# Selecting experts' tokens: counts of the later pairs through DRAM, the residual copied behind the first gathers, steps placed by distance

## The chip, the cores and the metric

The kernel runs on one core of a Trainium2 chip. A core has TensorE (PE), VectorE (DVE), ScalarE (ACT), GpSimd (POOL) and SyncE (SP), each with its own instruction stream, and 16 DMA engines that all queues share. The metric is device microseconds of one execution; less is better. Compared are medians of several executions.

## The reference

A block of three layers on x of 4 x 2048 tokens (8192 in all) of 256 floats: half of a mixture of experts, an attention, half of the same mixture of experts, each on the layer norm of x and added to x.

```python
x = x + 0.5 * ffn(layernorm(x));  x = x + attn(layernorm(x));  x = x + 0.5 * ffn(layernorm(x))

def ffn(x):                      # E = 8 experts, K = 2, capacity = 1.25 * 8192 / 8 = 1280
    probs = softmax(x @ router_w.T)
    topw, topi = top_k(probs, 2);  topw = topw / (sum(topw) + 1e-6)
    # of each expert's tokens the `capacity` with the largest weight are kept
    g, u = disp @ wg, disp @ wu  # per expert: 1280 x 256 @ 256 x 1024
    eo = (silu(g) * u) @ wd      # 1280 x 1024 @ 1024 x 256
    return sum over kept (token, expert) of weight * eo
```

The attention has 16 heads and is linear in the number of tokens (a context of keys and values, then queries times the context).

## The kernel before

**Stages.** A first router (layer norm, logits, the two best experts, their weights), then the first eight experts, the attention (with the second router's work in its last part), and the second eight experts. Each expert stage is `experts`, called twice.

**Experts.** An expert's 1280 tokens are two chunks of 640, so there are chunks 0 to 15; an even chunk is an expert's first half. For each chunk, tokens' rows are gathered from DRAM by five indirect DMAs of 128 rows (`gather`, L775, on GpSimd's queue), scaled on ScalarE (`norm`, L790; for chunk 0 on VectorE, L788), transposed (`turn`) and multiplied (`units`, TensorE at L899; then `down`, L1114) in a scheme with fewer block products and sums before and after, which run on VectorE (L840) and GpSimd (L843). Results are added to rows in DRAM by indirect DMAs (`send_tile`, L1048): into `acc` in the first stage, into the output in the second. `units` goes through four column blocks p = 0 to 3; near the third `ct` sum of each stands the place that the change calls "fifth", a little later (not for p = 3) the place "fourth", and `down` has one place, "end". Each place is a call of `aside`, which does one step of the pairs' work below. Before, "fifth" is used in odd chunks only.

**Which tokens an expert keeps.** Experts are treated in pairs. To find the 1280th largest weight of each of a pair's experts, a search with 7 + 7 rounds (`ROUNDS`, upper and lower half of the float's bits) compares 512 numbers of each partition to a threshold of that partition and counts. A partition is one of 8 `MARKS` groups (2 experts x 4 thresholds) of 16 partitions; the counts of a group's 16 partitions must be summed and be known on all partitions, as all derive the next thresholds from them. `Pair.steps` is a generator: each `yield` ends one step. A round is `sign` (ScalarE: signs of all keys less the threshold, summed per partition into `part`, a half float, L432) and `turn` (TensorE: `part` as a weight, broadcast, times the group matrix `own_b`, into a `reach` bank in PSUM, L436; VectorE: compare with `MOST_ABOVE` into `seen` and `ahead`, L437, and move the threshold `mark`, L440). After the rounds come the tail's steps: ties and larger ones (L496, L497), sums over partitions on TensorE (L505) and a scan on VectorE (L391), places (L509 to L514), a transpose back (`back`, L517) and the slots (L519, L486 to L488), from which the lists of rows are made.

The first pair (experts 0, 1) has its own code in `route`. The other three are `Pair`s 1 to 3 of `Others`, one after the other: 24 steps each, 72 in all. `route` does eight of them, `first_list` one and `first_turn` three; of the other 60, an expert's two chunks take twelve (four in the even chunk, eight in the odd one). The list of expert 2, the first of pair 1, is made in chunk 2, that of expert 4 in chunk 6, of expert 6 in chunk 10.

**Order.** Inside `tc.manual_schedule` the order on TensorE, VectorE, ScalarE (and GpSimd in the routers) is that of the code. SP is ordered by a planner. SP issues all plain loads and stores: x, the weights (`load_expert`: `wgt`, `wut`, `wdt`, 1 MB each, two experts' buffers), the rows and `acc`. Each DMA of SP also waits for the one that used its semaphore before. A DMA that waits holds up what is behind it on SP.

**The residual.** `acc` begins as a copy of x: four stores of 2 MB from `xw` in SBUF (L1622), three ahead of the rows' four stores (L388), one behind them; then `wdt` of expert 0 (`load_down`). The rows, 280 floats per token, are what the gathers read.

Of the kernel before, what the change touches and what calls it, by code (L numbers as in the profile page):

```python
# [20 lines left out]
P = 128  # L21
# [7 lines left out]
def macaron_kernel(  # L29
# [40 lines left out]
    acc = dram.tile([B * N, D], F32, name="acc")  # L70

# [85 lines left out]
    LONE = float(1 << 14)  # L157
    ACROSS = P * SEG

    def marks_of(name, weight, lacks):  # L160
# [13 lines left out]
    own_b = const.tile([P, MARKS + 1], F16, name="own_b")  # L174
    nc.gpsimd.memset(own_b, 0.0)
    nc.gpsimd.tensor_copy(own_b[:, :MARKS], heads[:, :: P // MARKS])
# [11 lines left out]
    rungs_a, rungs_b = (  # L188
        const.tile([P, len(UNITS), ROUNDS, MARKS + 1], F32, name=f"rungs_{k}") for k in "ab"
    )  # L190
    moves = const.tile([P, len(UNITS), ROUNDS + 2], F32, name="moves")
    for part, unit in enumerate(UNITS):
        strides = [unit * (COPIES + 1) ** (ROUNDS - 1 - n) for n in range(ROUNDS)] + [0.0]
        for n in range(ROUNDS):
            nc.gpsimd.memset(rungs_a[:, part, n, :], strides[n])
            nc.gpsimd.tensor_scalar(
                rungs_b[:, part, n, :MARKS], half_of[:, :: P // MARKS], strides[n], None, ALU.mult
            )
            nc.gpsimd.memset(moves[:, part, n : n + 1], strides[n + 1] - strides[n])
        nc.gpsimd.memset(moves[:, part, ROUNDS:], strides[0])  # L200
# [4 lines left out]
    nc.gpsimd.tensor_copy(rungs_b[:, :, :, MARKS:], moves[:, :, :ROUNDS].unsqueeze(3))  # L205
# [17 lines left out]
    shift = const.tile([P, T], F32, name="shift")  # L223
    slot_lo = const.tile([P, E, T], I16, name="slot_lo")
# [168 lines left out]
    class Pair:  # L393
# [4 lines left out]
        def use(self, pool, ppool, tag, bufs=1):  # L398
            self.pool, self.ppool, self.tag, self.bufs = pool, ppool, tag, bufs

# [25 lines left out]

        def steps(self):

            s, mark = self.s, self.s["mark"]

            def sign(key):
                nc.scalar.activation(self.junk, key, AF.Sign, bias=mark, scale=-1.0, accum_out=s["part"])  # L432

            def turn(half, n):
                reach = self.bank("reach")[:, : MARKS + 1]
                nc.tensor.matmul(reach, s["part"].to_broadcast([P, P]), own_b, start=True, stop=True)  # L436
                nc.vector.scalar_tensor_tensor(  # L437
                    s["seen"], reach, MOST_ABOVE, rungs_b[:, half, n, :], ALU.is_le, ALU.mult, accum_out=s["ahead"]
                )
                nc.vector.tensor_scalar(mark, s["ahead"], mark, None, ALU.add)  # L440

            es = slice(self.e - PAIR, self.e)
            w0 = self.key.rearrange("p (r m) -> p r m", r=QT)
            for e in range(PAIR):
                nc.scalar.copy(
                    w0.rearrange("p r (e g q) -> p r e g q", e=PAIR, g=COPIES)[:, :, e],
                    spread(
                        raw[:, self.e - PAIR + e, :].rearrange("p (q r) -> p r q", r=QT).unsqueeze(2),
                        [P, QT, COPIES, T // QT],
                    ),  # L450
                )
# [5 lines left out]
            nc.scalar.mul(self.key, low, UNITS[1])  # L457
            with nc.allow_low_precision(reason="sums of at most 512 signs are exact in half floats"):
                sign(upper)
                yield  # L460
                for n in range(ROUNDS - 1):
                    turn(0, n)
                    sign(upper)
                    yield
                turn(0, ROUNDS - 1)
                nc.vector.tensor_scalar(s["high"], mark, 0.5, None, ALU.add)
                yield
                nc.vector.tensor_scalar(s["top"], s["high"], float(1 << 16), None, ALU.mult)
                nc.vector.scalar_tensor_tensor(self.key, upper, s["high"], self.key, ALU.subtract, ALU.add)
                nc.vector.tensor_copy(mark, moves[:, 1, ROUNDS + 1 :])  # L470
                yield
                sign(self.key)
                yield
                for n in range(ROUNDS - 1):
                    turn(1, n)
                    sign(self.key)
                    yield
# [3 lines left out]
            yield  # L481
# [7 lines left out]
            yield  # L489

        def tail(self, wt):
# [6 lines left out]
            yield  # L498
# [9 lines left out]
            yield  # L508
# [6 lines left out]
            yield  # L515
# [6 lines left out]
            yield  # L522

    class Others:
# [8 lines left out]

        def step(self):
            next(self.left, None)

    def route(w, w0, pool, ppool, sums=iter(()), beside=iter(())):
# [51 lines left out]
        for n, _ in enumerate(first.tail(pair)):  # L589
            if n == 2:  # L590
# [128 lines left out]
    def load_down(e, weights):  # L719
        nc.sync.dma_start(out=weights[e][2], in_=wd[e].rearrange("(f p) d -> p f d", p=P))  # L720

    def load_expert(e, wpool, weights, behind=(), whole=True):
# [9 lines left out]
        if whole:  # L732
            load_down(e, weights)
# [22 lines left out]
    def experts(name, src, dst, wait_for, others, weights, ws, wpool, lpool, pool, ppool):  # L756
# [131 lines left out]
        def units(k):  # L888
# [82 lines left out]
            for p in range(NF):  # L971
# [13 lines left out]
                if k % PER:  # L985
                    aside(k)
                if not last:
# [11 lines left out]
                    aside(k)  # L999
# [40 lines left out]
        def aside(k):  # L1040

            others.step()
# [50 lines left out]
        def down(k, hs):  # L1093
# [56 lines left out]
            aside(k)  # L1150
# [29 lines left out]
        with tc.manual_schedule(engines=ENGINES - {mybir.EngineType.Pool}):  # L1180
# [402 lines left out]
    with tc.tile_pool(name="w1", bufs=2) as wpool:  # L1583
        weights, ws = {}, {}
        read = tc.alloc_tile_pool(name="read", bufs=1, side="right")
        with tc.tile_pool(name="r1", bufs=1) as pool, tc.tile_pool(name="r1p", bufs=2, space=PSUM) as ppool:
# [99 lines left out]
```

## Time and profile before

| what | us |
|---|---|
| median of three runs (lowest, highest) | 1976.41 (1975.58, 1977.82) |
| the profiled execution, its span | 1976.69, 1974.9 |
| first router and first lists, to the first product of chunk 0 (L899) | 0 to 96.2 |
| first expert stage, to the end of its last scatter-add | 96.2 to 893.4 |
| attention | to 1119.6 |
| second selection, to its first product | to 1169.0 |
| second expert stage | 1169.0 to the end |

The page's first part gives each engine's busy time, the fourth the chain of work that ended last. The granted TensorE clock is 0.971 of full on average. Windows give the busy time of each engine in a stretch; timelines the single instructions, with the idle time before and what ended it in square brackets. L numbers are lines of the kernel before.

### The profile page before, as it was taken

The numbers are of one execution on the slowest core, as the hardware profiler recorded it, in microseconds if no ns is written. First come the engines' busy times: TensorE is split into PE (matmuls) and PEld (weight loads), VectorE is DVE, ScalarE is ACT, GpSimd is POOL, SyncE is SP. The second block draws the span as 40 slices with busy tenths as digits, with TensorE's granted clock in tenths as the row PEclk, the third lists the DMA queues.
The fourth block names the chain that finished last, engine by engine and source line by source line (L and its number), as shares of the span: only waits on it lengthen the run. The fifth ranks groups of instructions, "written<-read, shape, count | busy, mean of one in ns | idle before, by whom it ended". The sixth has DMA issues, their size and how long they took to land.

```text
span 1974.9 us, 26091 instructions
## 1 busy us (share of the span) xinstructions
PE 1866.0 (94%) x8882; PEld 1338.4 (68%) x8882; DVE 1372.7 (70%) x2677; ACT 1030.4 (52%) x2598; POOL 1030.3 (52%) x1061
## 2 busy tenths in 40 slices
PE   7499999999999999999999659999999999999997
PEld 5366766676667777776888536666666666777776
DVE  8678677776777676646677667867686767676763
ACT  5273747374736463325566437374737473737332
POOL 6434555555555555535555435555545554555552
PEclk9599999999999999999999869999999999999999
DMA  9912232222222221115012541313131313132121
GB/s 346 308 50 75 46 74 47 71 50 71 50 71 50 71 50 28 29 22 178 22 43 90 201 160 18 92 25 96 22 90 26 95 26 88 30 96 28 31 28 19
DMA packets 108005, 148.90 MB, mean 75 GB/s; under 512 B 7512, under 2 KB 94560, under 8 KB 107872
## 3 DMA queue, kind: packets, MB, share of 16 engines
q1 hardware_dynamic: 76992, 103.16, 15.3%
q0 software_dynamic: 30720, 43.93, 13.7%
q8 instruction: 70, 1.15, 0.2%
q14 instruction: 63, 0.52, 0.1%
q10 hardware_dynamic: 160, 0.14, 0.1%
HBM read 91.11 MB, written 56.10 MB: 75 GB/s over the span
## 4 chain that ended last, share of the span: by engine, by line
PE 46%; DVE 4%; ACT 2%; issue 1%; POOL 1%; DMA 1%; POOLq 0%; SPq 0%; DVEq 0%; ACTq 0%
PE mm L899 23%; PE mm L1114 11%; PE py L1412 3%; PE pc L1354 3%; PE qp L1295 3%; DVE ct L840 1%; PE back L1066 1%; PE tr L801 1%; PE trq L1342 1%; DVE junk_a L562 1%; PE trx L1287 1%; DVE key L514 0%; PE ix L699 0%; ACT lo L693 0%; POOL out_dram L1048 0%
## 5 line engine op out<-in xcount | busy, mean ns | idle before, releaser
L899 PE MATMUL mm<-xs,ws 128*128 128x320 f32 x1536 | 479.3, 435 | 1.7 <-DVE u L840 1.7
L843 POOL TENSOR_TENSOR ct<-ct 128x320 f32<-128x320 f32 x360 | 337.0, 936 | 200.9 <-DVE ct L930 151.7
L899 PEld LDWEIGHTS mm<-xs,ws 128*128 128x128 f32 x1536 | 282.2, 190 | 116.8 <-DVE ct L840 6.6
L840 DVE TENSOR_TENSOR ct<-u,mm 128x640 f32<-128x640 f32 x256 | 209.5, 819 | 151.3 <-PE mm L899 110.5
L775 POOL DMA_INDIRECT r<-rows,ixs x160 | 156.6, 979 | 273.3 <-ACT eo L1047 197.1
L927 ACT ACTIVATE ct<-ct 128x960 f32<-128x960 f32 (+1 forms) x192 | 141.2, 735 | 299.2 <-DVE ct L840 285.9
L840 DVE TENSOR_TENSOR ct<-ct,mm 128x640 f32<-128x640 f32 x288 | 236.0, 819 | 72.9 <-PE mm L899 57.2
L1114 PE MATMUL mm<-ct,wds 128*128 128x320 f32 x960 | 279.6, 433 | 1.0 <-DVE ct L840 1.0
L693 ACT ACTIVATE lo<-from_below,behind_lo 128x129 f16<-128x129 f16 x896 | 272.8, 395 | 0.0
L1114 PEld LDWEIGHTS mm<-ct,wds 128*128 128x128 f32 x960 | 178.7, 190 | 75.0 <-DVE ct L840 7.0
L1114 PE MATMUL mm<-ct,wdt 128*128 128x320 f32 x720 | 217.2, 438 | 0.0
L1048 POOL DMA_INDIRECT acc<-eo,ixs x80 | 128.0, 1600 | 146.4 <-ACT eo L1047 128.4
L1048 POOL DMA_INDIRECT out_dram<-eo,ixs x80 | 127.9, 1599 | 146.3 <-ACT eo L1047 128.4
L899 PE MATMUL mm<-xsT,wgt 128*128 128x320 f32 x512 | 189.9, 453 | 3.0 <-ACT p L939 2.0
L899 PE MATMUL mm<-xsT,wut 128*128 128x320 f32 x512 | 179.6, 432 | 0.0
L930 DVE TENSOR_TENSOR ct<-ct 128x640 f32<-128x640 f32 (+1 forms) x128 | 158.1, 1235 | 22.0 <-ACT ct L927 22.0
L1114 PEld LDWEIGHTS mm<-ct,wdt 128*128 128x128 f32 x720 | 133.4, 193 | 49.3 <-issue 4.2
L840 DVE TENSOR_TENSOR u<-p,mm 128x640 f32<-128x640 f32 x126 | 103.4, 821 | 87.6 <-PE mm L899 56.1
L899 PE MATMUL mm<-xsT,ws 128*128 128x320 f32 x512 | 161.8, 439 | 2.4 <-DVE ct L840 2.4
L939 ACT COPY p<-mm 128x640 f32<-128x640 f32 x126 | 86.4, 686 | 90.1 <-PE mm L899 74.5
L899 PEld LDWEIGHTS mm<-xsT,ws 128*128 128x128 f32 x512 | 97.4, 191 | 43.9 <-DVE ct L840 4.3
L899 PEld LDWEIGHTS mm<-xsT,wut 128*128 128x128 f32 x512 | 97.3, 190 | 40.6 <-issue 0.2
(340 smaller groups left out, 2932.9 us busy)
## 6 DMA issues: line engine op xcount, KB each, us to landing
wgt<-in_L_ffn_wg_dram SPq DMA_DIRECT2D x16, 1024.0 KB
wut<-in_L_ffn_wu_dram SPq DMA_DIRECT2D x16, 1024.0 KB
wdt<-in_L_ffn_wd_dram SPq DMA_DIRECT2D x16, 1024.0 KB
rows<-xw SPq DMA_DIRECT2D x6, 2240.0 KB
xw<-in_L_attn_x_dram SPq DMA_DIRECT2D x16, 512.0 KB
acc<-xw SPq DMA_DIRECT2D x4, 2048.0 KB
out_dram<-xw SPq DMA_DIRECT2D x16, 512.0 KB
xw<-acc SPq DMA_DIRECT2D x15, 512.0 KB
```

Source lines behind the costliest of these rows:

```text
L693: nc.scalar.activation(lo[:, t, :], from_below, AF.Sign, bias=at, scale=1.0)
L775: gathers[k].append(nc.gpsimd.indirect_dma_start(out=r, out_offset=None, in_=src[:, :], in_offset=bass.IndirectOffsetOnAxis(ap=lists[e][:, ...
L840: nc.vector.tensor_tensor(o, a, b, op)
L843: nc.gpsimd.tensor_tensor(o, a, b, op)
L899: nc.tensor.matmul(ps, a, b, start=start, stop=True, skip_group_check=not start)
L927: nc.scalar.activation(h(p)[:, qs, :], h(p)[:, qs, :], AF.Silu)
L930: engine.tensor_tensor(h(p)[:, qs, :], h(p)[:, qs, :], hT(p)[:, qs, :], ALU.mult)
L939: nc.scalar.copy(p1, ps)
L1048: ins = nc.gpsimd.indirect_dma_start(out=dst[:, :], out_offset=bass.IndirectOffsetOnAxis(ap=lists[e][:, i0 + i : i0 + i + 1], axis=0), in_ ...
L1114: nc.tensor.matmul(ps, a(p), b(p), start=(p == 0 and not more), stop=(p == NF - 1), skip_group_check=more)
L1295: nc.tensor.matmul(qp[i][:, k, 0:W1], xT[i][:, k, c, :], wqx[:, c, :], start=(c == 0), stop=(c == DC - 1))
L1354: nc.tensor.matmul(pcs[b][:, c, 0 : D + 1], eks[i][:, k, c * P : (c + 1) * P], ring[i % 4][:, k, :], start=(first and k == 0), stop=(last ...
```

## The change

Of pairs 2 and 3 (`far`), a round's counts go another way: SP stores `part` (one half float of each of 128 partitions) into a DRAM tile `told`, then loads those 128 half floats to every partition, into `heard` (memory of `shift`, free at that time). `turn` sums them by groups on VectorE (into memory of `rstd`) and compares that sum, now in SBUF, instead of the PSUM bank. For pair 1 the matmul stays. A ninth column (`MARKS + 1`), which had carried the threshold's own move through the compare, is gone; the move is now a second operand of the instruction that moves `mark`. Two small set-up operations of GpSimd go with it.

Each `yield` now says how far off the next step should be (3, 7 or, after a far sign, 7.5), and `aside` knows each place's distance from the chunk's start (chunks counted as 49.0); a step is done at the first place that is not nearer than that. "fifth" is a place in all chunks. Two pairs of steps are joined (`low` with the copy, sums with places), so a pair has 23 steps.

`acc` is copied from x in DRAM to DRAM, four DMAs that wait for the gathers of chunk 0. The planner's order on SP is now: x and small weights; `wgt`, `wut`, `wdt` of expert 0; `wut`, `wdt` of expert 1; the rows' four stores; the four copies; `wgt` of experts 1 and 2; and from there stores and loads of `told` between the weights. Of the 28 rounds of a stage, those of pair 2 begin at the end of chunk 1 and finish in chunk 4, those of pair 3 run in chunks 6 to 9. In each stage the wait of `wdt` of experts 3 and 5 stands ahead of one store of `told` (those after the steps at the "end" of chunks 3 and 7).

```diff
+    told = dram.tile([1, P], F16, name="told")
...
+    ROUND = 7.5
...
+    heard = shift.bitcast(F16)[:, :P]
...
+        def far_step(self):
+            return ROUND if self.called else 3
+
         def steps(self):
 
             s, mark = self.s, self.s["mark"]
+
+            def reached():
+                if not self.called:
+                    reach = self.bank("reach")[:, :MARKS]
+                    nc.tensor.matmul(reach, s["part"].to_broadcast([P, P]), own_b, start=True, stop=True)
+                    return reach
+                reach = rstd[:, :MARKS]
+                nc.vector.tensor_reduce(reach, heard.rearrange("p (m k) -> p m k", m=MARKS), AX.X, ALU.add)
+                return reach
 
             def sign(key):
                 nc.scalar.activation(self.junk, key, AF.Sign, bias=mark, scale=-1.0, accum_out=s["part"])
+                self.called = self.far
+                if self.far:
+                    nc.sync.dma_start(out=told.rearrange("o p -> p o"), in_=s["part"])
+                    nc.sync.dma_start(out=heard, in_=told[0, :].partition_broadcast(P))
 
             def turn(half, n):
-                reach = self.bank("reach")[:, : MARKS + 1]
-                nc.tensor.matmul(reach, s["part"].to_broadcast([P, P]), own_b, start=True, stop=True)
                 nc.vector.scalar_tensor_tensor(
-                    s["seen"], reach, MOST_ABOVE, rungs_b[:, half, n, :], ALU.is_le, ALU.mult, accum_out=s["ahead"]
+                    s["seen"][:, :MARKS], reached(), MOST_ABOVE, rungs_b[:, half, n, :], ALU.is_le, ALU.mult,
+                    accum_out=s["ahead"],
                 )
-                nc.vector.tensor_scalar(mark, s["ahead"], mark, None, ALU.add)
+                nc.vector.tensor_scalar(mark, s["ahead"], mark, moves[:, half, n : n + 1], ALU.add, ALU.add)
...
-                yield
+                    yield self.far_step()
...
             scan(place, tie)
-            yield
             nc.vector.tensor_copy(nums, cnt)
...
+        def start(self):
+            self.due = 0.0
+            for pair in self.pairs[1:]:
+                pair.far = True
+
         def step(self):
-            next(self.left, None)
+            return next(self.left, None)
+
+        def step_at(self, at):
+            if at >= self.due:
+                self.due = at + (self.step() or 0.0)
...
-                if k % PER:
-                    aside(k)
+                aside(k, "fifth", p)
...
-        def aside(k):
+        PLACES = {"fifth": (7.3, 15.2, 23.2, 31.0), "fourth": (10.6, 18.6, 26.6), "end": (45.8,)}
+
+        def aside(k, place, p=0):
 
-            others.step()
+            others.step_at(k * 49.0 + PLACES[place][p])
...
             if 1 not in weights:
+                for b in range(B):
+                    some = slice(b * N, (b + 1) * N)
+                    after(nc.sync.dma_start(out=acc[some, :], in_=x_rows[some, :]), gathers[0], "the first rows come first")
                 load_expert(1, wpool, weights, gathers[0])
             first_turn()
+            others.start()
...
-            load_expert(0, wpool, weights, whole=False)
+            load_expert(0, wpool, weights)
...
-                batches = [slice(b * NJ, (b + 1) * NJ) for b in range(B)]
-                for n, b in enumerate(batches[: B - 1] + batches + batches[B - 1 :]):
-                    if B - 1 <= n < 2 * B - 1:
-                        write_rows(xw, rows[0], b)
-                    else:
-                        nc.sync.dma_start(out=acc_tiles[:, b, :], in_=xw[:, b, 0:D])
-                load_down(0, weights)
+                for b in range(B):
+                    write_rows(xw, rows[0], slice(b * NJ, (b + 1) * NJ))
```

More of the change, by code (lines that the diff above doesn't have):

```diff
@@ L173, in macaron_kernel @@
     marks_a = marks_of("a", LONE, (-(CAP - 1.0) * LONE / ACROSS,) * 2)
-    own_b = const.tile([P, MARKS + 1], F16, name="own_b")
-    nc.gpsimd.memset(own_b, 0.0)
-    nc.gpsimd.tensor_copy(own_b[:, :MARKS], heads[:, :: P // MARKS])
+    own_b = const.tile([P, MARKS], F16, name="own_b")
+    nc.gpsimd.tensor_copy(own_b, heads[:, :: P // MARKS])
     MOST_ABOVE = B * N - 2.0 * CAP + 1.0
@@ L187, in macaron_kernel @@
     nc.vector.tensor_reduce(which, inside, AX.X, ALU.add)
-    rungs_a, rungs_b = (
-        const.tile([P, len(UNITS), ROUNDS, MARKS + 1], F32, name=f"rungs_{k}") for k in "ab"
-    )
+    rungs_a = const.tile([P, len(UNITS), ROUNDS, MARKS + 1], F32, name="rungs_a")
+    rungs_b = const.tile([P, len(UNITS), ROUNDS, MARKS], F32, name="rungs_b")
     moves = const.tile([P, len(UNITS), ROUNDS + 2], F32, name="moves")
@@ L196, in macaron_kernel @@
             nc.gpsimd.tensor_scalar(
-                rungs_b[:, part, n, :MARKS], half_of[:, :: P // MARKS], strides[n], None, ALU.mult
+                rungs_b[:, part, n, :], half_of[:, :: P // MARKS], strides[n], None, ALU.mult
             )
@@ L204, in macaron_kernel @@
     )
-    nc.gpsimd.tensor_copy(rungs_b[:, :, :, MARKS:], moves[:, :, :ROUNDS].unsqueeze(3))
     for part, unit in enumerate(UNITS):
@@ L399, in use @@
             self.pool, self.ppool, self.tag, self.bufs = pool, ppool, tag, bufs
+            self.far = False
         def bank(self, name):
@@ L451, in steps @@
                 )
-            yield
+            yield 7
             high, low = self.copies(w0, self.bank("copies"))
@@ L455, in steps @@
             nc.scalar.copy(upper, high)
-            yield
             nc.scalar.mul(self.key, low, UNITS[1])
+            yield 3
             with nc.allow_low_precision(reason="sums of at most 512 signs are exact in half floats"):
                 sign(upper)
-                yield
+                yield self.far_step()
                 for n in range(ROUNDS - 1):
@@ L463, in steps @@
                     sign(upper)
-                    yield
+                    yield self.far_step()
                 turn(0, ROUNDS - 1)
                 nc.vector.tensor_scalar(s["high"], mark, 0.5, None, ALU.add)
-                yield
+                yield 3
                 nc.vector.tensor_scalar(s["top"], s["high"], float(1 << 16), None, ALU.mult)
@@ L470, in steps @@
                 nc.vector.tensor_copy(mark, moves[:, 1, ROUNDS + 1 :])
-                yield
+                yield 3
                 sign(self.key)
-                yield
+                yield self.far_step()
                 for n in range(ROUNDS - 1):
@@ L476, in steps @@
                     sign(self.key)
-                    yield
+                    yield self.far_step()
                 turn(1, ROUNDS - 1)
@@ L480, in steps @@
             nc.vector.tensor_tensor(s["cand"], s["cand"], s["top"], ALU.bitwise_or)
-            yield
+            yield 3
             ps = self.bank("pair")[:, :P]
@@ L488, in steps @@
             nc.scalar.activation(behind_lo[:, es], slot_lo[:, es], AF.Identity, bias=a_half, scale=-1.0)
-            yield
+            yield 3
         def tail(self, wt):
@@ L497, in tail @@
             nc.vector.tensor_scalar(above, wt, cand, 0.0, ALU.is_gt, ALU.add, accum_out=parts[:, 0:1])
-            yield
+            yield 7
             cnt = self.bank("all")[:, :2]
@@ L507, in tail @@
             scan(place, tie)
-            yield
             nc.vector.tensor_copy(nums, cnt)
@@ L514, in tail @@
             nc.vector.scalar_tensor_tensor(place, place, off, above, ALU.add, ALU.mult)
-            yield
+            yield 7
             ps = self.bank("back")[:, :P]
@@ L521, in tail @@
             )
-            yield
+            yield 3
     class Others:
@@ L589, in route @@
         for n, _ in enumerate(first.tail(pair)):
-            if n == 2:
+            if n == 1:
                 others.step()
@@ L717, in end, with load_expert @@
             return ix
-    def load_down(e, weights):
-        nc.sync.dma_start(out=weights[e][2], in_=wd[e].rearrange("(f p) d -> p f d", p=P))
-    def load_expert(e, wpool, weights, behind=(), whole=True):
+    def load_expert(e, wpool, weights, behind=()):
         if e >= E:
@@ L731, in load_expert @@
         weights[e] = wgt, wut, wdt
-        if whole:
-            load_down(e, weights)
+        nc.sync.dma_start(out=wdt, in_=wd[e].rearrange("(f p) d -> p f d", p=P))
     NF = FC // 2
@@ L998, in units @@
                     silu(p, slice(1, 4))
-                    aside(k)
+                    aside(k, "fourth", p)
                     if not ahead:
@@ L1149, in down @@
             sums_of_x(k + 1)
-            aside(k)
+            aside(k, "end")
             p4 = banks()[:, 0, :BH]
```

## The prediction

> **What bounds the kernel now.** I read the page first: span 1974.9 us, and the profiled execution took 1976.69 us, 0.28 over the median of 1976.41; so the sum below starts from 1976.7.
>
> ```profile
> PE 1866.0 (94%) x8882; PEld 1338.4 (68%) x8882; DVE 1372.7 (70%) x2677; ACT 1030.4 (52%) x2598; POOL 1030.3 (52%) x1061
> ...
> PE 46%; DVE 4%; ACT 2%; issue 1%; POOL 1%; DMA 1%; POOLq 0%; SPq 0%; DVEq 0%; ACTq 0%
> PE mm L899 23%; PE mm L1114 11%; PE py L1412 3%; PE pc L1354 3%; PE qp L1295 3%; DVE ct L840 1%; PE back L1066 1%; PE tr L801 1%; PE trq L1342 1%; DVE junk_a L562 1%; PE trx L1287 1%; DVE key L514 0%; PE ix L699 0%; ACT lo L693 0%; POOL out_dram L1048 0%
> ```
>
> TensorE carries the two expert stages. A change to the later pairs' steps counts only by the TensorE time it takes, or by making TensorE wait. To price the steps I laid four chunks side by side in the windows view, each from the middle of one down product to the middle of the next (chunks 4, 5, 12, 13 of the first stage; columns: TensorE, its weight load, VectorE, ScalarE, GpSimd busy, clock, DMA share, GB/s).
>
> ```profile
> 286.41:335.67 49.26, 48.66 (x193) 33.83 (x193) 36.78 (x61) 30.87 (x83) 27.07 (x23) 1.00 0.24 50
> 335.67:388.20 52.53, 50.61 (x266) 34.96 (x265) 38.28 (x72) 25.80 (x65) 26.05 (x23) 1.00 0.27 67
> 686.90:734.55 47.65, 47.65 (x189) 33.61 (x188) 35.43 (x52) 28.06 (x75) 27.35 (x23) 1.00 0.25 52
> 734.55:783.58 49.03, 49.03 (x254) 34.68 (x254) 31.72 (x44) 23.71 (x59) 26.85 (x23) 1.00 0.17 29
> ```
>
> The last two have no steps: TensorE never idles, 47.65 us for an even chunk, 49.03 for an odd one. Measured so (by the starts of the copy at L1133), chunks 1 to 9 of the first stage exceed these by 3.50, 0.65, 1.13, 1.61, 3.48, 0.74, 1.15, 1.61, 5.17 = 19.0 us, those of the second by 20.5. This 39.5 us is all that steps cost there. Most lies in the three chunks per stage that end a pair (25.9 us in six). The timelines of VectorE, GpSimd and TensorE show how:
>
> ```profile
> 175.38 1.11 DVE L391 TENSOR_TENSOR_SCAN key<-ones,scratch 128x128 f32<-128x128 f32 x1
> 176.53 2.79 DVE L514 SCALAR_TENSOR_TENSOR key<-key,nums_b,scratch 128x128 f32<-128x128 f32 x1
> ```
> ```profile
> 176.16 3.01 POOL L930 TENSOR_TENSOR ct<-ct 128x1280 f32<-128x1280 f32 x1
> ```
> ```profile
> 179.38 0.33 PE L517 MATMUL back<-ident,key 128*128 128x128 f32 x1 [1.52 <-DVE key L514]
> 180.11 1.34 PE L899 MATMUL mm<-xsT,ws 128*128 128x320 f32 x4 [0.41 <-DVE ct L840]
> ```
>
> VectorE takes `key` beside GpSimd and needs 2.79 us (0.35 in the first pair's tail, with GpSimd idle); the transpose of it is the next step, 3 us later in TensorE's order, so TensorE waits 1.52 + 0.41. In three of the six the next six matmuls then took 3.0 instead of 1.6 us, with the granted clock at 0.50: an idle of 2 us can cost 1.5 more.
>
> A count on TensorE costs little: the eight of chunk 3 cost 1.13 us, 0.14 each.
>
> **The change, part by part.**
>
> *Counts through DRAM.* Pairs 2 and 3 have 14 rounds each, so 28 per stage leave TensorE, 56 in all: 56 x 0.14 = 7.9 us less. Added: 112 DMAs on SP, and on VectorE 56 reductions of 128 half floats (nearest row, a reduction of 128x128 to 16 columns, 0.24 to 0.29 us). VectorE is 74% busy in a chunk with steps; chunk 3 shows eight turns of 0.45 us hidden, so 0.3 more hides, if the data is there.
>
> Is it there? The next turn stands on VectorE behind the third `ct` sum of the next column block: 304.73, 312.55, 320.37, 328.87 in chunk 4. Reduction, compare, read and add take 0.85, the sign on ScalarE 0.9 (0.71 + 0.19), which leaves 7.8 - 1.9 = 5.9 us for both transfers. No row shows a 2-byte store. From below: the 8 KB read of `wr`, issued at 0.79, is used at 2.55, 1.76 us; twice that is 3.5. From above: the last scatter-add into `acc`, issued at 889.70, lets SP go at 893.51 (3.8), and the 256 KB read issued then is used at 896.37 (2.9); together 6.7. Much of the upper end is descriptor writing on GpSimd (1.56) and volume, so I take 4.7, nearer the lower end: 1.2 us to spare, no wait. At the upper end VectorE waits 0.8 in each of the 16 rounds per stage whose next turn is one place on, and all that is queued behind it with it (the `ct` sums that free TensorE's banks): up to 26 us.
>
> SP runs in order. The scheduled order puts the down weights of experts 3 and 5 ahead of one store each (waiting for the end of the odd chunk, then 1 MB, 3 us at the 300 GB/s of that stretch); the next turn is 10.5 us on. 0 to 2 us each, four in all; I take 1 together. No weight load is late for it: they are used a chunk later.
>
> *The compare's new input.* `seen` read PSUM and took 158 to 168 ns in all 84 runs. Now both inputs are in SBUF, as in L514 and L391, which the rows above show stretched beside GpSimd. At the first three places GpSimd issues DMAs or waits; at the fourth it runs L930 (2.9) and L843 (0.93 each): about five rounds per stage meet it. Bounds 0 and 2.9 each; nearest is one L843, half of it on average: 0.5 x 10 = 5 us of VectorE time, half of it passed to TensorE: 2.5.
>
> On "SBUF — State Buffer", section "Who interferes with whom", the Trainium skill says the same in general: a VectorE instruction with two SBUF inputs waits out a GpSimd instruction that reads SBUF, one with a single input does not. It speaks against this edit; by its full block of one L843 at each of the ten the sum would be some 2.5 us longer, and without any block 2.5 shorter.
>
> *Steps by distance.* Tail steps now stand 7 us apart, so `back` no longer meets its own `key`: the 1.5 + 0.4 wait and the clock's 1.5 go. What is late next is VectorE itself: scan, `nums`, mask, scan and `key` are one step, 2.1 us with GpSimd idle (0.42 + 0.15 + 0.35 + 0.23 + 0.15 + 0.42 + 0.35), up to 5.7 as in the rows above. Pair 1's falls at the start of chunk 1, pair 2's before GpSimd's block in chunk 5, pair 3's in chunk 9 beside L843. TensorE keeps 0.5 us of its own (transposes, sums); between 0.5 and the old 3.5 I take 1.7 per tail: 25.9 - 6 x 1.7 = 15.7 saved. It holds the two copy steps of the next pair (0.43 of transposes) in the same chunks.
>
> Even chunks now take five steps instead of four and sign before the copy that TensorE waits for (0.35 us in chunk 4, behind ScalarE's row scaling): 1.5 each for four chunks per stage against 4.6 and 4.5 for the four before: +2.9. Odd chunks 3 and 7 go from 1.14 to 0.8: -1.3. Chunk 0 takes eight steps of pair 1, still on TensorE, instead of four: 4 x 0.14 and a sign of 0.9 in the way, part of it hidden: +1.0 per stage. The removed matmuls and the 2.5 of blocking are inside these chunk figures. Together -15.7 + 2.9 - 1.3 + 2.0 = -12.1.
>
> *Residual.* Before, the store of `acc`'s last quarter and 1 MB of `wdt` follow the rows on SP; the first gathers, issued at 84.33, run beside them. Stage 2 shows gathers with nothing beside them.
>
> ```profile
> 84.33 1.26 POOL L775 DMA_INDIRECT r<-rows,ixs  x1 [20.24 <-DVE mark_b L470]
> ...
> 92.05 1.53 DVE L788 TENSOR_SCALAR r<-r 128x256 f32<-128x256 f32 x3 [7.95 <-DMA r<-rows,ixs]
> ...
> 1162.07 1.11 POOL L775 DMA_INDIRECT r<-rows,ixs  x1 [12.15 <-ACT behind_lo L657]
> ...
> 1165.05 0.41 DVE L788 TENSOR_SCALAR r<-r 128x256 f32<-128x256 f32 x1 [2.00 <-DMA r<-rows,ixs]
> ```
>
> 7.7 against 3.0 us. The rows' store still starts at 54.1: it waits for GpSimd at L380, and the queue had been empty since 52, after 6.3 MB of `acc`, in whose place now stand 3 MB of weights (`wdt` of expert 0, `wut` and `wdt` of expert 1). So the gathers start no earlier. From issue to the first count of chunk 0 on TensorE it is 23.7 against 20.6, to the first product 11.9 against 6.9: 3.1 to 5.0 saved, I take 3.5.
>
> In exchange 8.4 MB from DRAM to DRAM start at about 92, beside the second chunk's gathers (issued 90.9 to 96.0). At the 345 GB/s of the rows' store it ends after 24 us, at twice the traffic after 49: 116 to 141. ScalarE scales those rows at 117.89, 114.4 in the new time, and all its later copies queue behind that. GpSimd's first scatter-add (146.1, so 142) waits for the copy too; the gathers behind it (155, used at 168) have room. `wgt` of expert 1, last on SP, is not read before 187. The first gathers' rows came only when the other queue's 3 MB had drained; by that row the second ones wait for the copy: 2 to 27 us. If they slip between, 0. I take 3, near the lower bound: the weights' 4 KB pieces move at 408 to 418 GB/s in their windows, the copy's are 64 KB. Sum: -0.5.
>
> The Trainium skill, "DMA: Bandwidth & Descriptors", "Queues, rings and completion order", says that an engine alternates between its queues packet by packet; by that the gathers would slip between and the sum were 3 us lower. The row does not look like fair turns.
>
> **Sum:** 1976.7 - 12.1 + 1.0 (rounds behind a load) - 0.5 = 1965. A difference below 0.2% (4 us) is about what cannot be told from none here.
>
> **Rivals.**
> - *The rounds are late* (slower). Nothing in the trace times a store of 128 two-byte pieces. If sign to sum takes 8 us instead of the 4.7, 2.1 us of wait fall on 32 tight rounds, 67 us, of which 20 to 60 reach TensorE: 1985 to 2025. It decides from a round of about 6.3 us on, where 32 x 0.4 eats the gain. Against it: both upper rows contain work that the rounds lack.
> - *The copy holds the second gathers.* 8 us and more, at the upper bound 27, instead of 3: 1970 to 1989. For it the first gathers' 7.7 us, against it the higher rate of larger pieces.
> - *Everything hides:* tails at 0.7 (-6), no blocking (-2.5), the second gathers slip through (-3), even chunks at 1.0 (-4): 1950.
>
> **How the numbers follow.** Forecast 0.50 (1955 to 1973), late rounds 0.17, held gathers 0.19, everything hides 0.14. Below 1972.5: 0.46 of the first, 0.03 of the third, all of the last, 0.63. Within 0.2%: 0.04 + 0.09 + 0.01 = 0.14. Above: 0.23. The range leaves out the far half of the late rounds and the lowest few us: 1949 to 1990.
>
> **What would show it.** Chunks 1, 5 and 9 fall to 50 to 51 us, even far chunks stay near 49; VectorE's new reduction waits less than 0.3 us on its DMA; `seen` at the fourth place is longer than 0.17; the first rows are used 3 us after their gather; ScalarE waits at its first scaling of the second chunk's rows for 2 us or more. Reductions that wait over 1 us on DMA, or a chunk 0 that is 10 us longer, make the prediction wrong.

## The result, and the profile after

The changed kernel takes 2757.8 us (2755.4 to 2759.5) against 1977.1 (1975.6 to 1978.8): 1.395 times as long, 95% interval 1.392 to 1.397. The forecast was 1965, and the range ended at 1990.

The page of the changed kernel: the lines of busy time, the granted clock in 40 slices, and the two lines of the chain that ended last.

```profile
PE 1991.8 (72%) x8826; PEld 1412.1 (51%) x8826; DVE 1378.4 (50%) x2733; ACT 1036.8 (38%) x2598; POOL 1022.8 (37%) x1059
...
PEclk8897777797776899999999797777796776799999
...
PE 23%; DMA 22%; DVE 3%; issue 2%; ACT 2%; POOL 1%; another core or an unknown queue 0%; POOLq 0%; DVEq 0%; ACTq 0%; SPq 0%
DMA told<-part_b 17%; PE mm L919 10%; DMA shift<-told 5%; PE mm L1135 5%; PE qp L1320 2%; PE py L1437 2%; PE pc L1379 2%; ACT scratch L445 1%; PE trx L1312 0%; DVE ct L860 0%; PE trq L1367 0%; PE back L1087 0%; DVE junk_a L586 0%; DVE mark_b L456 0%; PE tr L821 0%
```

TensorE was busy for 94% of the span and is so for 72%. The chain names the cause at once: the store of the 256 bytes of `told` carries 17% of it, the load of them 5%. The clock row is lower where TensorE idles: mostly 0.7 through the far chunks, 0.9 and more in most of the rest. The span is 780.6 us longer; 125.8 of that is TensorE's longer busy time (1991.8 against 1866.0, with fewer matmuls), 654.8 its idle time.

Next the windows of chunks 4, 5, 12 and 13 of the first stage, cut as in the prediction (columns: TensorE, its weight load, VectorE, ScalarE, GpSimd busy, clock, DMA share, GB/s):

```profile
398.64:519.85 121.21, 60.92 (x190) 40.78 (x189) 35.54 (x66) 31.89 (x85) 26.30 (x23) 0.75 0.21 22
519.85:579.12 59.27, 51.36 (x262) 35.94 (x261) 35.66 (x64) 25.34 (x63) 26.84 (x23) 0.94 0.25 60
1071.86:1119.51 47.65, 47.65 (x189) 33.55 (x188) 35.47 (x51) 27.95 (x74) 27.36 (x23) 1.00 0.25 52
1119.51:1168.55 49.04, 49.01 (x254) 34.71 (x253) 31.70 (x45) 23.80 (x59) 26.86 (x23) 1.00 0.18 29
```

Chunks without steps are what they were (47.65, 49.04). Chunk 4, wholly in pair 2's rounds, takes 121 us instead of 49. Chunk 1, which has pair 1's tail and no far round, takes 50.3 instead of 52.5. So the loss lies where the rounds through DRAM are.

The waits, of VectorE, then of SP's queue, then of ScalarE, then of TensorE (total us, times, longest):

```profile
DVE rstd L441 <- DMA shift<-told: 658.5, 55, 17.9
```
```profile
SPq L449 <- DMA told<-part_b: 917.5, 54, 20.2
```
```profile
ACT scratch L445 <- DVE mark_b L456: 667.6, 58, 19.4
```
```profile
PE mm L919 <- ACT p L959: 339.2, 28, 17.8
PE mm L1135 <- DVE ct L860: 132.5, 12, 14.1
```

55 of the 56 reductions wait for the load, 12 us each. On SP the load waits 17 us for the store that it reads from. TensorE is named with other releasers only because `p` and `ct` stand behind the turn: `ct` on VectorE itself, `p` on ScalarE behind the next sign (L445), which waits for the turn's `mark_b`. One round in full, first SP, then VectorE:

```profile
237.44 0.32 SPq L448 DMA_DIRECT2D told<-part_b  x1
254.67 0.32 SPq L449 DMA_DIRECT2D shift<-told  x1
```
```profile
259.52 0.28 DVE L441 TENSOR_REDUCE rstd<-shift 128x8 f32<-128x128 f16 x1 [13.16 <-DMA shift<-told]
```

Store to load 17.2 us, load to reduction 4.9: 22 us, where I had taken 4.7 for both. Over all 56 rounds the first has a median of 17.3 (14.5 to 20.6), the second of 5.0. The DMA view of that same store, of 238.20 to 238.45, counts its packets (queue, packets, MB, share of 16 engines), and the windows behind it (columns as above) show that no other traffic is in its way:

```profile
q1 hardware_dynamic: 144, 0.00, 30.9%
```
```profile
245.00:250.00 5.00, 3.73 (x14) 2.28 (x12) 1.10 (x2) 0.70 (x3) 0.00 (x0) 1.00 0.00 0
250.00:254.60 4.60, 0.00 (x0) 0.00 (x0) 0.00 (x0) 0.00 (x0) 0.00 (x0) 0.95 0.00 0
```

All 144 packets of the store (the 128 pieces and 16 more) are on record within this quarter of a microsecond, 0.8 to 1.0 us after its issue; so by these records the 16 us that follow are not the DMA engines' time for the pieces. From 245 on the windows read DMA share 0.00 and 0 GB/s: no packet is on record for any of the sixteen engines, and SP still waits for the store's end. This already tells against one rival, that the store queues behind weights or gathers. What it waits for was to be found: the 128 pieces go into the same 256 bytes.

### The profile page after: what moved, and what is told of

The parts are those of the page before. It is cut to its first block, busy times and chain, and to the rows that moved or that the text cites. A ratio compares the mean times of both kernels' runs of the same rounds, so it can differ in the third digit from the quotient of the medians.

```text
span 2755.5 us, 26223 instructions
## 1 busy us (share of the span) xinstructions
PE 1991.8 (72%) x8826; PEld 1412.1 (51%) x8826; DVE 1378.4 (50%) x2733; ACT 1036.8 (38%) x2598; POOL 1022.8 (37%) x1059
## 4 chain that ended last, share of the span: by engine, by line
PE 23%; DMA 22%; DVE 3%; issue 2%; ACT 2%; POOL 1%; another core or an unknown queue 0%; POOLq 0%; DVEq 0%; ACTq 0%; SPq 0%
DMA told<-part_b 17%; PE mm L919 10%; DMA shift<-told 5%; PE mm L1135 5%; PE qp L1320 2%; PE py L1437 2%; PE pc L1379 2%; ACT scratch L445 1%; PE trx L1312 0%; DVE ct L860 0%; PE trq L1367 0%; PE back L1087 0%; DVE junk_a L586 0%; DVE mark_b L456 0%; PE tr L821 0%
## 5 line engine op out<-in xcount | busy, mean ns | idle before, releaser
L919 PE MATMUL mm<-xs,ws 128*128 128x320 f32 x1536 | 517.3, 462 | 86.1 <-DVE u L860 73.7
L919 PE MATMUL mm<-xsT,wgt 128*128 128x320 f32 x512 | 212.8, 501 | 354.9 <-ACT p L959 339.2
L919 PEld LDWEIGHTS mm<-xs,ws 128*128 128x128 f32 x1536 | 307.3, 206 | 217.9 <-DVE u L860 78.3
L1135 PE MATMUL mm<-ct,wds 128*128 128x320 f32 x960 | 301.9, 461 | 132.5 <-DVE ct L860 132.5
L441 DVE TENSOR_REDUCE rstd<-shift 128x8 f32<-128x128 f16 x56 | 16.0, 286 | 658.5 <-DMA shift<-told 658.5
L919 PEld LDWEIGHTS mm<-xsT,wgt 128*128 128x128 f32 x512 | 97.0, 210 | 408.5 <-ACT p L959 363.5
L1135 PEld LDWEIGHTS mm<-ct,wds 128*128 128x128 f32 x960 | 192.1, 204 | 216.6 <-issue 148.5
L919 PE MATMUL mm<-xsT,wut 128*128 128x320 f32 x512 | 200.7, 477 | 0.0
L445 ACT ACTIVATE scratch<-upper,mark_b 128x512 f16<-128x512 int16 x42 | 30.3, 722 | 356.2 <-DVE mark_b L456 316.8
L445 ACT ACTIVATE scratch<-key,mark_b 128x512 f16<-128x512 f32 x42 | 30.2, 719 | 353.7 <-DVE mark_b L456 350.9
```

The costliest lines, as they stand in the source:

```text
L919: nc.tensor.matmul(ps, a, b, start=start, stop=True, skip_group_check=not start)
L1135: nc.tensor.matmul(ps, a(p), b(p), start=(p == 0 and not more), stop=(p == NF - 1), skip_group_check=more)
```

## The experiments

The runs below come from four chips, each with its own runs of the kernel before, whose median differed by chip (1972 to 1979 us), so ratios are compared.

### The other two parts

`e1_near`: the far way is never taken.

```diff
             self.due = 0.0
-            for pair in self.pairs[1:]:
-                pair.far = True
```

> The changed kernel with the counts of pairs 2 and 3 left on TensorE; the spacing of the steps and the copy of the residual stay. Theory (the round through DRAM is the whole loss, the other two parts gain): 1962 us, 1955 to 1970; chunks 1, 5 and 9 of both stages at 49.5 to 51 us. Rival (the spacing or the copy also cost): 1977 or more.

Measured: 1966.3 us against 1978.8, ratio 0.993 (0.992 to 0.994). All of the loss is the far way; spacing and copy together gain.

`e2_residual`: the kernel before with only the copy, and the order on SP that belongs to it.

```diff
-                batches = [slice(b * NJ, (b + 1) * NJ) for b in range(B)]
-                for n, b in enumerate(batches[: B - 1] + batches + batches[B - 1 :]):
...
-                load_down(0, weights)
+                for b in range(B):
+                    write_rows(xw, rows[0], slice(b * NJ, (b + 1) * NJ))
...
+                for b in range(B):
+                    some = slice(b * N, (b + 1) * N)
+                    after(nc.sync.dma_start(out=acc[some, :], in_=x_rows[some, :]), gathers[0], "the first rows come first")
```

> The kernel before with the residual's copy alone (and the order of weights and rows on SP that goes with it). Theory: the first rows are used 3 us after their gather instead of 7.7, and the second gathers slip through beside the copy: 1 to 4 us faster, 1972.5 to 1976. Rival (the copy delays something in chunk 0 by as much as the earlier start gives): 1976 to 1980.

Measured: 1976.4 against 1978.8, ratio 0.999 (0.998 to 1.000): 2.4 us less, within the theory's 1 to 4, but in microseconds among the rival's 1976 to 1980, with single runs from 1973.1 to 1982.8: not to be told from none.

### Why the store takes 17 us

`e3_spread`: the same store and load, but each piece in a row of its own, 512 bytes apart. TensorE supplies the values, VectorE waits for the load as before. (In this run and the others that leave gaps, one more store fills `told` at the start of a stage.)

```diff
-    told = dram.tile([1, P], F16, name="told")
+    told = dram.tile([P, 2 * P], F16, name="told")
...
-                    nc.sync.dma_start(out=told.rearrange("o p -> p o"), in_=s["part"])
-                    nc.sync.dma_start(out=heard, in_=told[0, :].partition_broadcast(P))
+                    nc.sync.dma_start(out=told[:, :1], in_=s["part"])
+                    nc.sync.dma_start(out=heard, in_=told[0, :P].partition_broadcast(P))
```

> Counts on TensorE again, so that values are right; the store and the load of each far round remain, and VectorE still waits for the load and sums what it brings, without use. The 128 two-byte pieces go to 128 different rows of 512 bytes, and the load reads the first 256 contiguous bytes. Theory (pieces that go into the same 256 bytes of DRAM are done one after the other): the store falls from 17 us to 2 to 4, the kernel to 2030 to 2150. Rival (a piece of two bytes is slow wherever it goes): the store stays at 15 to 20, the kernel at 2740 to 2790.

Measured: 1970.1 us, ratio 0.995 (0.994 to 0.997). The store falls from 17.3 to 1.5 us, and the loss is gone; the theory had the store right and expected too little of it, since the whole round now fits. The addresses made the difference between 1970 and 2758: the number of pieces, their size, the queue and the two DMAs of a round are the same (the load is as long, from the first row), and TensorE even has its 56 matmuls back.

`e4_half`: the pieces next to each other as in the change, half of them.

```diff
-                    nc.sync.dma_start(out=told.rearrange("o p -> p o"), in_=s["part"])
+                    nc.sync.dma_start(out=told[:, : P // 2].rearrange("o p -> p o"), in_=s["part"][: P // 2])
```

> As the last one, but with the pieces in the same 256 bytes as in the changed kernel, and only those of partitions 0 to 63 are stored. Where the time goes by pieces (same place or small size): the store falls from 17 us to 8 to 10, the kernel to 2250 to 2400. Rival (a fixed time of the store, or of the queue's waits): 15 to 20 as before, the kernel at 2740 to 2790.

Measured: 2292.9 us, ratio 1.158 (1.156 to 1.160); the store takes 9.2 us (8.5 to 12.1). One of its rounds on SP:

```profile
240.08 0.45 SPq L448 DMA_DIRECT2D told<-part_b  x1
249.30 0.32 SPq L449 DMA_DIRECT2D shift<-told  x1
```

If the time goes in a straight line with the pieces, 17.3 and 9.2 us for 128 and 64 of them make 0.126 us a piece and 1.2 us besides. No fixed time of a store explains that.

`e5_stride4`: all pieces, 4 bytes apart, and a load of the whole 512 bytes (into the memory of `rstd` and `shift` together; the sums go into `seen`), so that the counts go the far way alone.

```diff
-    told = dram.tile([1, P], F16, name="told")
+    told = dram.tile([P, 2], F16, name="told")
...
-                nc.vector.tensor_reduce(reach, heard.rearrange("p (m k) -> p m k", m=MARKS), AX.X, ALU.add)
+                nc.vector.tensor_reduce(reach, heard[:, ::2].rearrange("p (m k) -> p m k", m=MARKS), AX.X, ALU.add)
```

> The changed kernel with one difference in the way of the counts: the pieces lie 4 bytes apart (512 bytes in all), the load brings all 512 bytes and VectorE sums every second half float. TensorE has no part in the far counts, as in the changed kernel. From the half run a piece costs 0.126 us behind one that goes to the same place, plus 1.2 us. What is 'the same place'? If 64 bytes: 16 pieces in each, the store takes 1.2 + 16 x 0.126 = 3.2 us, the round about 7 to 8 us where 5.9 are free: 1975 to 2030. If 256 bytes: 9.3 us, 2250 to 2300. If the whole 512 bytes or more: 17.3 us, 2740 to 2790. If no more than 4 bytes: 1.5 us, 1958 to 1968.

Measured: 2185.9 us, ratio 1.108 (1.107 to 1.110), the store 7.5 us (6.6 to 9.5). It lies between the values for places of 64 and of 256 bytes and meets neither; my picture of pieces that wait strictly in turn within a place of fixed size is too simple.

`e7_stride16` and `e8_stride64`: as `e3_spread`, 16 and 64 bytes apart; the diff is that of the first, the other has `P // 4` in place of 8.

```diff
-    told = dram.tile([P, 2 * P], F16, name="told")
+    told = dram.tile([P, 8], F16, name="told")
```

> As the run with the pieces 512 bytes apart (values from TensorE, VectorE waits for a load of 256 contiguous bytes), but the pieces 16 bytes apart, 2 KB in all. Stores so far: 17.3 us for 128 pieces in 256 bytes, 9.2 for 64 pieces in 128, 7.5 for 128 in 512, 1.5 for 128 in 64 KB. If pieces wait for each other inside a place of about 200 to 256 bytes (some 50 in turn in the last but one): 16 pieces in turn, 1.2 + 16 x 0.126 = 3 us, and the kernel 1985 to 2030. If the whole tile is the place, however long: 17 us and 2750. If 64 bytes apart are needed and less does not help: 7 or more, above 2180.

> The same with the pieces 64 bytes apart, 8 KB in all. By a place of 200 to 256 bytes: 4 pieces in turn, 1.5 to 1.9 us, the kernel 1970 to 1978, as with 512 bytes. If pieces must lie a whole 512 bytes apart to be free of each other: 3 us or more, the kernel above 1985.

Measured: both 0.995 (0.993 to 0.997), 1962.6 and 1962.2 us, both lower than expected; the store takes 2.3 and 1.7 us. In `e8_stride64` the trace also has the landings (KB, median us from issue to landing):

```profile
told<-part_b SPq DMA_DIRECT2D x56, 0.2 KB, 1.9
shift<-told SPq DMA_DIRECT2D x56, 32.0 KB, 2.9
```

Its store of 226.23, too, has all 144 packets on record within 0.3 us (227.0 to 227.3); SP goes on at 227.67. So the packets pass as fast in both runs, and the difference comes behind them.

| run | pieces | bytes apart | issue of store to issue of load, median us (range) | ratio to before |
|---|---|---|---|---|
| the change | 128 | 2 | 17.3 (14.5 to 20.6) | 1.395 |
| `e4_half` | 64 | 2 | 9.2 (8.5 to 12.1) | 1.158 |
| `e5_stride4` | 128 | 4 | 7.5 (6.6 to 9.5) | 1.108 |
| `e7_stride16` | 128 | 16 | 2.3 (1.4 to 3.9) | 0.995 |
| `e8_stride64` | 128 | 64 | 1.7 (1.4 to 3.4) | 0.995 |
| `e3_spread` | 128 | 512 | 1.5 (1.4 to 3.4) | 0.995 |

So the cause is settled as far as it bears on the kernel: a store of two-byte pieces ends late when they lie close together in DRAM. `e5_stride4`, where TensorE takes no part and little but the distance and the length of the load differs from the change, shows it too. What happens behind the engines is not on record, and the size of the place within which pieces hold each other up is not settled; the table falls smoothly.

### What the change would be with a quick store

`e9_ideal`: pieces 64 bytes apart, no matmul for the far counts, everything else as changed. It leaves out the gathering of the pieces: what VectorE sums are not the counts.

```diff
-    told = dram.tile([1, P], F16, name="told")
+    told = dram.tile([P, P // 4], F16, name="told")
...
-                    nc.sync.dma_start(out=told.rearrange("o p -> p o"), in_=s["part"])
-                    nc.sync.dma_start(out=heard, in_=told[0, :].partition_broadcast(P))
+                    nc.sync.dma_start(out=told[:, :1], in_=s["part"])
+                    nc.sync.dma_start(out=heard, in_=told[:4, :].rearrange("m k -> (m k)").partition_broadcast(P))
```

> The changed kernel with the pieces 64 bytes apart and a load of 256 contiguous bytes, and no matmul for the far counts: what the change would be if its store were not slow. The numbers that VectorE sums are then not the counts, so experts 4 to 7 keep other tokens than they should; every instruction is still done. Theory (the forecast of 1965 out of 1976.7, ratio 0.994, failed at the round through DRAM alone): 0.988 to 0.993 of the kernel before, and below the run with the same pieces and the matmuls (0.9947) by up to 8 us. Rival (VectorE's compare of two SBUF inputs or the rounds' waits eat what the matmuls free): 0.994 or more.

`e10_near2`, `e11_spacing2` and, on another chip, `e6_spacing`: the near counts again, and the spacing without the copy (the stores of `acc` and `load_down` of the kernel before put back into `e1_near`).

```diff
+                batches = [slice(b * NJ, (b + 1) * NJ) for b in range(B)]
...
+                load_down(0, weights)
-                for b in range(B):
-                    write_rows(xw, rows[0], slice(b * NJ, (b + 1) * NJ))
```

> All counts on TensorE and the residual stored from SBUF as before; only the spacing of the steps (with the joined steps, the new places and the threshold's move as a second operand) is left of the change. Theory (the three parts add): the 1966.3 of spacing and copy together plus the 2.4 that the copy alone gave, 1966 to 1971. Rival (the copy gives nothing, or takes): 1962 to 1966.

> Again all counts on TensorE with spacing and copy (0.9929 on another chip), to stand beside the others of this call: 0.991 to 0.995.

> Again the spacing alone (0.9930 on another chip). If the copy gives nothing, it is level with the last run within 0.1%; if the copy gives the 4 to 6 us by which chunk 0 starts its first down product earlier in the traces, it is 4 to 6 us slower than that.

| run | us | ratio to before (95%) |
|---|---|---|
| `e9_ideal`: far counts, quick store, spacing, copy | 1965.1 | 0.996 (0.994 to 0.997) |
| `e10_near2`: near counts, spacing, copy | 1956.4 | 0.992 (0.990 to 0.993) |
| `e11_spacing2`: near counts, spacing | 1960.0 | 0.993 (0.991 to 0.994) |
| `e6_spacing`, the same on another chip | 1960.7 | 0.993 (0.992 to 0.994) |

`e6_spacing` lies below both of its forecasts, which came from times of a slower chip (1978.8 against 1973.8 before); its ratio is that of spacing and copy together, as its rival had it. `e11_spacing2` is 3.5 us slower than `e10_near2`, between its two cases, and the intervals overlap. So what the copy gives stays open.

The theory for `e9_ideal` fell: it is not below 0.993, where the rival had 0.994 or more, and it is 8.7 us slower than near counts on the same chip. No reduction waits for its load any more, so the rounds are in time. Its chunks without steps take what they take elsewhere, so the other tokens of experts 4 to 7 do not show. Yet the windows of its chunks 4 and 5 (columns as above) read

```profile
281.85:332.40 50.55, 49.05 (x189) 33.06 (x189) 37.93 (x72) 30.71 (x82) 27.52 (x23) 1.00 0.25 52
332.40:382.58 50.18, 49.80 (x261) 34.64 (x261) 35.92 (x64) 25.80 (x65) 27.16 (x23) 1.00 0.28 70
```

against 47.66 and 48.79 for its chunks without steps. The tail's chunk is short, the even chunk is not. The timelines of ScalarE and TensorE show one cause, once in each even far chunk:

```profile
518.81 0.71 ACT L445 ACTIVATE scratch<-key,mark_b 128x512 f16<-128x512 f32 x1
519.42 0.20 ACT L445 ACTIVATION_READ_ACCUMULATOR scratch<-key,mark_b 128x1 f16 x1
519.52 0.68 ACT L960 COPY p<-mm 128x640 f32<-128x640 f32 x1
```
```profile
520.25 0.81 PE L920 MATMUL mm<-xsT,wgt 128*128 128x320 f32 x2 [1.02 <-ACT p L960]
```

The sign stands ahead of the copy `p` that TensorE waits for, and costs 1.02 us. In `e8_stride64`, with the matmuls, the same wait is 0.90; there chunks 1 to 9 of the first stage exceed 47.65 and 48.79 by 15.6 us in all, without the matmuls by 17.3 (measured here and below between the second copies of the down products, which the signs do not shift). So taking the 56 matmuls off TensorE brought nothing that shows. In `e10_near2` it is 12.7: spaced by 3 instead of 7.5, the steps are done early in chunk 8, and chunk 9 is bare. The difference, 4.6 here and 4.4 in the second stage, is about the 8.7 us.

`e12_later`: the copy waits for the second chunk's gathers too.

```diff
-                    after(nc.sync.dma_start(out=acc[some, :], in_=x_rows[some, :]), gathers[0], "the first rows come first")
+                    after(nc.sync.dma_start(out=acc[some, :], in_=x_rows[some, :]), gathers[1], "the first rows come first")
```

> All counts on TensorE, spacing, and the copy, which here waits for the gathers of chunk 1 as well (issued until 97). In two traces with the copy VectorE and ScalarE stood 3 to 4 us around 95 to 99, just after it began. If the copy's traffic is the cause, that stand is gone and chunk 0's first down product begins at 131 to 132 instead of 134.3: up to 3 us below the run before last. If not, no difference.

Measured: 1955.2 us, ratio 0.991 (0.989 to 0.992), the fastest of all, but within the intervals of `e10_near2`. Its reason can't be shown: the stand at 95 to 99 is missing in `e10_near2` as well, in the same kernel that had it as `e1_near`, and the first copy of the first down product is at 132.4 and 132.1. The stand looked like this in the changed kernel's ScalarE:

```profile
98.10 0.69 ACT L959 COPY y<-mm 128x640 f32<-128x640 f32 x1 [4.32 <-remote]
```

Stands of this kind cost TensorE 2.28 us there, 2.06 in `e1_near`, 1.72 in `e3_spread` and 1.87 in `e4_half`. No trace without the copy has one, and of those with it none from the other chips. What the unnamed releaser is, and why it went by the chip, stays open.

## Why the prediction was wrong

**The step that failed** is "Is it there?", in the counts through DRAM, where the round told plus heard was put at "4.7, nearer the lower end: 1.2 us to spare, no wait". The upper bound, 6.7, was none for this store. The bounds came from an 8 KB read, a scatter-add of whole rows and a 256 KB read, and I judged the store by its bytes. None of these rows has 128 pieces going into the same 256 bytes, and that is what takes the time: 17.3 us for the store, 5.0 for the load and its wait, 22 us in all. I wrote that nothing in the trace timed such a store, and yet let rows that are unlike it close the range above.

For pieces that lie apart the 4.7 was right: in `e8_stride64` the landings are 1.9 us for the store and 2.9 for the load, 4.8 together. The time available was at least that, as no reduction waits in `e8_stride64`, `e3_spread` and `e9_ideal`; in `e7_stride16`, with 2.3 and 3.4 in the median, two wait, 0.3 us in all, which fits the 5.9. (The 1.9 taken off there is 0.15 more than the 0.85 and 0.9 that it names.)

**The rival "the rounds are late"** had the mechanism and the side, with a chance of 0.17, and stopped at a round of 8 us. Its own working, 32 tight rounds times (22.2 - 5.9), would give 522 us, and 913 if all 56 were tight. The waits of VectorE add up to 658: 43 of 11 to 18 us, 11 of 7 to 9.4, one of 2.3 and one round without. TensorE's idle time grows by about as much (654.8), and with its slower matmuls the loss is 780.

Of the signs that the prediction named, chunk 1 fell to the 50 to 51 us it gave and the first rows were used 3 us after their gather; chunks 5 and 9, which also hold waits of far rounds, took 59.3 and 73.2, and "Reductions that wait over 1 us on DMA" was the one that told it wrong.

**Tails** were right in kind and came out a little shorter: the three chunks of the first stage that end a pair lost 3.5, 3.5 and 5.2 us to steps before, and 0.9, 1.4 and 1.7 in `e9_ideal` (over 47.65 and 48.79). I had 1.7 for each.

**Even far chunks** were put at 1.5 us; in `e9_ideal` they cost 2.9 (50.5 to 50.6 against 47.65). Of that TensorE idles 1.5 in chunk 4, 1.02 of it for the sign ahead of `p`, which I had priced at 0.35; and it is busy 1.4 longer, which I can't divide further.

**Matmuls off TensorE**, 7.9 us: not seen, as above. Chunk 3, where no compare is stretched, takes 49.27 us in `e8_stride64` with four far matmuls and 49.47 in `e9_ideal` without them; TensorE is busy 49.27 and 49.36. So the 0.14 per step that I read off chunk 3 was not the price of its matmul. That reading was loose besides: between second copies the old chunk 3 costs 1.74 us, not 1.13.

**The compare of two SBUF inputs** was a matter of eight compares, not ten, each 0.36 us longer. In `e9_ideal` 48 take 0.17 us and eight 0.52 to 0.53, and all eight stand at the last "fifth" place of an even chunk, the fourth of the prediction's four places, where a `ct` sum of GpSimd runs; the two turns at that place of odd chunks are not stretched:

```profile
325.09 0.52 DVE L452 SCALAR_TENSOR_TENSOR seen_b<-rstd,rungs_b 128x8 f32<-128x8 f32 x1
```
```profile
324.73 1.80 POOL L864 TENSOR_TENSOR ct<-ct 128x320 f32<-128x320 f32 x2
```

That is 2.9 us of VectorE instead of 5. With the input in PSUM none of the 84 is stretched in `e8_stride64`. The two sums of GpSimd take 1.80 together, so the first ends near 325.6, and the compare ends at 325.61: it waited out one GpSimd instruction. That is the Trainium skill's rule ("SBUF — State Buffer", "Who interferes with whom"), and this trace agrees with it, at a price of 0.36 each since the sum was half over.

**Residual:** the start was right and larger. The first gather, issued at 84.35, is used 3.1 us later instead of 7.7, and the first product comes 4.8 us earlier (91.43 against 96.19):

```profile
87.44 0.41 DVE L808 TENSOR_SCALAR r<-r 128x256 f32<-128x256 f32 x1 [3.00 <-DMA r<-rows,ixs]
```

The 3 us for second gathers held by the copy were wrong, but not because the copy lets them through. Their issues with the median us to landing, first from `e10_near2`, where the copy starts beside them, then from `e12_later`, where it waits for them:

```profile
r<-rows,ixs POOLq DMA_INDIRECT x5, 12.6
```
```profile
r<-rows,ixs POOLq DMA_INDIRECT x5, 4.0
```

The last of the five lands 22.3 us after its issue in `e10_near2`, at 118.8, when the copy ends as well (its last packet starts at 118.3; I had 116 to 141), and 3.4 us after it, at 99.7, in `e12_later`. So they are held as the row of the first gathers had it, and the last is late by far more than the 3 us. It costs nothing because I had all five needed at 114.4. ScalarE scales the tiles one by one, in `e10_near2` four from 114.08 and the fifth at 123.65, and each has landed by then, the fourth 3.0 us before. In the changed kernel, whose trace has no landings, ScalarE does not idle before them either:

```profile
115.99 2.08 ACT L810 ACTIVATE r<-r 128x256 f32<-128x256 f32 x4
```

The Trainium skill ("DMA: Bandwidth & Descriptors", "Queues, rings and completion order") has an engine take turns between its queues packet by packet. That the gathers would therefore slip between was my inference, and these landings tell against it; the copy's packets are 64 KB each (16 of them are 1.05 MB in the DMA view of `e10_near2`). In the kernel before, the gathers issued from 84.33 on have no packet on record up to 89.9, while SP's queue has 1866. No run here times a single turn. The copy brings 2.4 us in `e2_residual` and 3.5 between `e11_spacing2` and `e10_near2`, where I had 0.5; the interval of the first reaches 1.000, and those of the other two overlap.

**Chunk 0** with eight steps: 1.0 us per stage was forecast. With spacing alone the first copy of its down product comes 2.8 us later than before in `e11_spacing2` (137.69 against 134.89), 0.45 of which is a later first product (96.64 against 96.19): 2.35; in `e6_spacing` it is 3.3 less 0.8, 2.5. These are traces of different chips.

Without the store's 17 us the change is `e9_ideal`, 1965.1 us against 1973.7, 8.5 less, where my sum had 11.7 less. The other terms were off on both sides, and that they nearly made up for one another was luck.

## What to carry to other kernels

The time of this small DMA was not set by its bytes: before two bytes each of 128 partitions go side by side into DRAM, price the pieces, and where no row of the profile has pieces like them, leave the upper bound open. Pieces 16 bytes apart or more were harmless here; next to each other they cost 0.126 us each. This cross-partition sum, cheap on TensorE, had nothing to win by a way through DRAM, even with a quick store; what was worth having in this change is to space the steps by distance (0.993 alone), and perhaps the copy behind the first gathers (0.991 to 0.992 with it).

## What the runs showed of the hardware

- A store of 128 two-byte pieces to DRAM lasted 17.3 us where the pieces touch, 7.5 at 4 bytes apart, 2.3 at 16, 1.7 at 64 and 1.5 at 512; with half the pieces, touching, 9.2. In the first case and at 64 bytes apart all 144 packets of a store were on record within 0.3 us; behind them the DMA share read 0.00 while SP waited for the touching pieces, so a wait for a store can be long with all DMA engines at rest.
- With waits of about 12 us the granted clock was 0.75 on average in chunk 4, and TensorE was busy 60.9 us where a bare chunk takes 47.65 at the full clock; over the kernel its slower work added 126 us to 655 of idling, a fifth more.
- Beside a copy of 8.4 MB from DRAM to DRAM, in packets of 64 KB, five gathers landed 12.6 us after their issue in the median and 22.3 at most (`e10_near2`); ahead of it 4.0, and 3.4 for the last (`e12_later`). The rows were needed late enough that it cost nothing.
